# Last expert layer: rows of the routed tiles moved between partition quarters by plain transfers and transposed by VectorE in 32x32 blocks

## The chip, the cores and the metric

The kernel runs on one core of one Trainium2 chip. The metric is the device time of one execution in microseconds. Of the kernel before, four runs are given: 1134.13, 1129.19, 1130.49 and 1135.69 us, with a median of 1132.31 us. One more execution was profiled; it took 1130.32 us.

A core has five engines that run side by side, each with its own queue of instructions: TensorE (PE, matrix products and transposes into PSUM), VectorE (DVE), ScalarE (ACT), GpSimd (POOL) and SyncE (SP). Work passes between them by semaphores. Sixteen DMA engines move data between HBM and SBUF or inside SBUF. Transfers are issued from SP's queue, or, where rows are picked by an index, from POOL's.

## The reference

The program is two decoder layers of a gated cross-attention model on x of shape (4, 512, 512) in float32, that is 2048 tokens of width 512. Each layer adds a gated cross-attention and then a gated mixture of experts, both on a layer norm of x. Only the second mixture of experts, the last step, is touched by the change. Cut to what matters:

```python
x = hidden_states.reshape(-1, 512)                 # 2048 tokens
probs = softmax(x @ router_w.T)                    # 8 experts
topk_w, topk_idx = top_k(probs, 2)
topk_w = topk_w / sum(topk_w)
combine = zeros((2048, 8)).at[token, topk_idx].add(topk_w)
for e in range(8):                                 # gw, uw: 512 x 352, dw: 352 x 512
    out = silu(x @ gw[e]) * (x @ uw[e]) @ dw[e]
    acc = acc + combine[:, e, None] * out
shared = silu(x @ s_gate_w + b) * (x @ s_up_w + b) @ s_down_w + b
result = acc + shared
```

So each token goes through two of eight experts, and through a shared expert beside them. The kernel computes a token only at its two experts.

## The kernel before

**How the layer is tiled.** The 4096 pairs of token and expert are sorted by expert on the chip, and each expert's list is cut into tiles of 128 rows. `NTS` = 36 tiles are computed in a fixed loop; three more (`NT4` = 39) stand behind a branch that is taken only if the routing needs them. Which tokens a tile holds is known only at run time, so its rows are fetched by index: `gat4` holds the row numbers, `put4` the places where the results go.

**A tile's steps.** `rows4(i)` has POOL gather 128 rows of 512 values from HBM (`h4_dram`, the normed x) into the tile `xr`. A product on TensorE needs the 512 values along the partitions, so `in4(i)` transposes: the helper `transposed` runs four 128x128 transposes on TensorE into the PSUM tile `ptr` (L245) and copies them with one ScalarE instruction into `xrT` (L246). `up4(i)` multiplies `xrT` with the gate and the up weights (`pgr` and `pur`, L1443; four chunks of 128 each, which the profile shows as eight matmuls of 352 columns), takes silu on ScalarE (L1445) and multiplies on VectorE with the token's weight (`sgr`, L1446). `turn4(i)` transposes the result on TensorE (`pti`, L1454). `down4(i)` multiplies with the down weights (`por`, L1463), adds half the shared expert's bias on VectorE (`yr`, L1465) and scatters the rows from POOL (L1466).

**Weights.** Three buffers (`NW` = 3) hold an expert's gate, up and down weights (`wbuf`). `weights4(i)` gathers them from POOL by index in two transfers of 128 rows, of 11.3 KB and of 6.1 KB. Where tile i has the same expert as tile i - 3, the index lies out of bounds and nothing is moved.

**What sets the order.** TensorE and VectorE follow the order of the program text in this stage (a schedule by hand); the order on POOL, ScalarE and SP comes from a scheduler when the kernel is built, and is fixed from then on. In iteration i of the loop TensorE gets `up4(i + 1)`, the transposes of `in4(i + 2)`, `down4(i)` and `turn4(i + 1)`. Ahead of the loop stand the gathers of tiles 0 to 3, `in4(0)`, `up4(0)`, the third weight buffer, `in4(1)` and `turn4(0)`. SP issues nothing between the read of the slot table (`tab`, L1401) and the load of the shared expert's second half (L716, L717) at the end of the loop. After the loop come the sums of each token's two rows (L1517) and the rest of the shared expert (L1201, L1217).

**Memory.** Tiles come from pools. `row` buffers (nine of 2 KB per partition) hold `xr` and `yr`; `xrT` has three buffers. The pool `c4` holds, for the stage between the two expert layers, seven buffers `yk` of the first layer's gathered rows and the keys and values `kb` and `vb`; `wd2` and `half_db` take `yk` buffers over.

**Weight layout.** On the host `k_major` lays a weight out so that partition p of chunk c holds input value 128 c + p, to match the transposes.

Of the kernel before, what the change touches and what calls it, by code (L numbers as in the profile page):

```python
# [9 lines left out]
F32 = mybir.dt.float32  # L10
# [7 lines left out]
P = 128  # L18
B, S, D = 4, 512, 512
T = B * S  # L20
NT = T // P
TB = S // P
DC = D // P
N = 64
KSET = 4
HEADS = 16
HD = D // HEADS
# [6 lines left out]
E1, I1 = 8, 352  # L34
NT4 = (2 * T + E1 * (P - 1)) // P
NTS = 2 * T // P + E1 // 2
# [4 lines left out]
NROW = 9  # L41
NYK = 7
NW = 3
WROW = 2 * DC * I1
# [21 lines left out]
def flamingo_gated(  # L66
# [8 lines left out]
    nc = tc.nc  # L75
    V, A, G, PE = nc.vector, nc.scalar, nc.gpsimd, nc.tensor
# [4 lines left out]
    work = ctx.enter_context(tc.tile_pool(name="work", bufs=2))  # L81
# [9 lines left out]
    h4_dram = dram.tile([T, D], F32, name="h4_dram")  # L91
# [27 lines left out]
    for g in range(B):  # L119
# [22 lines left out]
        out=tri, in_=ones, compare_op=ALU.is_gt, fill=0.0, base=0,  # L142
# [98 lines left out]
    def transposed(dst, src, name, part=slice(0, P)):  # L241

        pt = ps_t.tile([P, DC, P], F32, name=name, tag="pt")
        for c in range(DC):
            PE.transpose(pt[:, c, :], src[:, c * P : (c + 1) * P], ident)  # L245
        A.copy(dst, pt[:, :, part])  # L246
# [479 lines left out]
    weights, rows0, xbTs, sgs, its = {}, {}, {}, {}, {}  # L726
# [128 lines left out]
    for i in range(NT2):  # L855
# [4 lines left out]
        k = i // 4 + 2  # L860
# [25 lines left out]
    c4 = ctx.enter_context(tc.tile_pool(name="c4", bufs=1))  # L886


    sm4 = ctx.enter_context(tc.tile_pool(name="sm4", bufs=2))


    TURN = [2, 0, 3, 1]
# [26 lines left out]
    for h in range(2):  # L919
        G.affine_select(  # L920
            out=cmask[h * N : (h + 1) * N, :], in_=ones[h * N : (h + 1) * N, :N], compare_op=ALU.is_ge,
# [22 lines left out]
        )  # L944

    def fetch(t, k):
        yk = c4.tile([P, D], F32, name=f"yk{t}_{k}", tag="yk", bufs=NYK)
        G.indirect_dma_start(  # L948
            out=yk,
            out_offset=None,  # L950
            in_=y_dram[:, :],
            in_offset=bass.IndirectOffsetOnAxis(ap=rows_of[:, t, k : k + 1], axis=0),
            bounds_check=NSLOT + P - 1,
            oob_is_err=False,
        )
        return yk
# [128 lines left out]


    def keys3(b):
        kb = c4.tile([P, DC, 4, N], F32, name=f"kb{b}", tag="kb", bufs=2)
        vb = c4.tile([P, HEADS // 2, 2, HD], F32, name=f"vb{b}", tag="vb", bufs=2)
        nc.sync.dma_start(out=kb, in_=kblk[b])  # L1090
        nc.sync.dma_start(out=vb, in_=vblk[b])
        return kb, vb

    pairs3 = [(2 * pair, 2 * pair + 1) for pair in range(2)]
    kv3 = {b: keys3(b) for b in pairs3[0]}
    loop.close()
    by_hand.close()
# [142 lines left out]
    def step(gen, n=1):  # L1240
        for _ in range(n):
            next(gen)
# [135 lines left out]
    def gather(out_, src, idx, n):  # L1378
        G.indirect_dma_start(
            out=out_,  # L1380
            out_offset=None,
            in_=src[:, :],
            in_offset=bass.IndirectOffsetOnAxis(ap=idx, axis=0),
            bounds_check=n - 1,
            oob_is_err=False,
        )
# [4 lines left out]
    def weights4(i):  # L1391
        wgu, wd = views4(at4[i])
        gather(wgu.rearrange("p a c i -> p (a c i)"), wgu1, wrow[:, i : i + 1], E1 * P)
        gather(wd.rearrange("p c d -> p (c d)"), wd1, wrow[:, i : i + 1], E1 * P)
# [13 lines left out]
    gat4 = c4.tile([P, NT4], I32, name="gat4")  # L1408
# [7 lines left out]
    run(d1)  # L1416


    wd2 = c4.tile([P, D], F32, name="wd2", tag="yk", bufs=NYK)
    nc.sync.dma_start(out=wd2, in_=wsd1[IS[0] + 2 * P :, :])  # L1420
    half_db = c4.tile([P, D], F32, name="half_db", tag="yk", bufs=NYK)
    nc.sync.dma_start(out=half_db, in_=sdb1.partition_broadcast(P))
    V.tensor_scalar(half_db, half_db, gf[:, 1:2], 0.5, ALU.mult, ALU.mult)

    xrs, xrTs, sgs, its = {}, {}, {}, {}

    def rows4(i):
        xrs[i] = work.tile([P, D], F32, name=f"xr{i}", tag="row", bufs=NROW)  # L1430
        gather(xrs[i], h4_dram, gat4[:, i : i + 1], T)

    def in4(i):
        xrTs[i] = work.tile([P, DC, P], F32, name=f"xrT{i}", tag="xnT", bufs=3)
        transposed(xrTs[i], xrs.pop(i), f"ptr{i}")

    def up4(i):
        (wgu, _), xbT = views4(at4[i]), xrTs.pop(i)
        pg = ps.tile([P, I1], F32, name=f"pgr{i}", tag="g")
        pu = ps.tile([P, I1], F32, name=f"pur{i}", tag="u")  # L1440
        for a, p_ in enumerate((pg, pu)):
            for c in range(DC):
                PE.matmul(p_, lhsT=xbT[:, c, :], rhs=wgu[:, a, c, :], start=(c == 0), stop=(c == DC - 1))  # L1443
        sg = work.tile([P, 512], F32, name=f"sgr{i}", tag="sg")
        A.activation(sg[:, :I1], pg, AF.Silu)  # L1445
        V.scalar_tensor_tensor(sg[:, :I1], pu, slots[:, 1, i : i + 1], sg[:, :I1], ALU.mult, ALU.mult)  # L1446
        sgs[i] = sg
# [28 lines left out]
        tc.add_to_no_dep_group("y4", d.ins)  # L1476

    after = [shared4(1, W5, g, wd2) for g in range(B)]
    for i in range(4):
        rows4(i)  # L1480
    in4(0)
    up4(0)
    weights4(NW - 1)
    in4(1)
    turn4(0)
    for i in range(NTS):
        if i + 1 < NTS:
            up4(i + 1)
        if i + 2 < NTS:
            in4(i + 2)  # L1490
        if i + 4 < NTS:
            rows4(i + 4)
        if i + 1 == NTS:
            step(after[0])
        down4(i)
        if i + NW < NTS:
            weights4(i + NW)
        elif i + NW == NTS:
            load_shared4(1, W5)
        if i + 1 < NTS:  # L1500
            turn4(i + 1)
# [20 lines left out]
def _host_layout(i):  # L1522
    import numpy as np

    def k_major(w):
        w = np.asarray(w)
        *lead, k, m = w.shape
        w = w.reshape(*lead, k // P, P, m)
        return np.ascontiguousarray(np.moveaxis(w, -3, -2))

    def t(w):
        return np.swapaxes(np.asarray(w), -1, -2)

    def beside(g, u):
        return np.concatenate([t(g), t(u)], axis=-1)

    def by_chunk(v):
        v = np.asarray(v)
        v = np.concatenate([v[: IS[0]], v[IS[0] - P // 2 :]])
        return np.ascontiguousarray(v.reshape(2, 3, P).transpose(2, 0, 1))  # L1540

    def shared1(part):
        return np.stack([k_major(np.asarray(i[f"L1_ffn_s_{n}_w"])[:, part]) for n in ("gate", "up")], axis=1)

    c = np.ascontiguousarray
    ctxs = np.asarray(i["ctx_2048"])

    kblk = np.zeros((B, 4, HD, DC, 4, N), ctxs.dtype)
    vblk = np.zeros((B, 2, N, HEADS // 2, 2, HD), ctxs.dtype)
    for j in range(4):  # L1550
        kblk[:, j, :, :, j] = ctxs.reshape(B, N, DC, 4, HD)[:, :, :, j].transpose(0, 3, 2, 1)
    for j in range(2):
        vblk[:, j, :, :, j] = ctxs.reshape(B, N, HEADS // 2, 2, HD)[:, :, :, j]
    kblk = kblk.reshape(B, P, DC, 4, N)
    vblk = vblk.reshape(B, P, HEADS // 2, 2, HD)
    return {
        "x": c(np.asarray(i["x"]).reshape(T, D)),

        "xT": c(np.asarray(i["x"]).reshape(B, TB, P, DC, P).transpose(1, 4, 3, 0, 2).reshape(B, P, DC, S)),
        "ctx": c(ctxs),  # L1560
        "kblk": c(kblk),
        "vblk": c(vblk),
        "itok": c(np.asarray(i["itok_Sx4_0_63"])),
        "g_xattn": c(np.asarray(i["g_xattn"])),
        "g_ffn": c(np.asarray(i["g_ffn"])),
        "descT": k_major(t(i["L0_xattn_desc_router"])),
        "w_q": c(np.asarray(i["L0_xattn_W_q"])),
        "b_q": c(np.asarray(i["L0_xattn_b_q"]).reshape(DC, P).T),
        "gate0T": k_major(t(i["L0_ffn_gate_w"])),
        "bias0": c(np.asarray(i["L0_ffn_bias"])),  # L1570
        "wgu0": k_major(beside(i["L0_ffn_w_gate"], i["L0_ffn_w_up"])),
        "wd0": k_major(t(i["L0_ffn_w_down"])),
        "wsgu0": k_major(beside(i["L0_ffn_sg"], i["L0_ffn_su"])),
        "wsd0": k_major(t(i["L0_ffn_sd"])),
        "gate1T": k_major(t(i["L1_ffn_router_w"])),
        "wgu1": c(
            np.stack([k_major(i["L1_ffn_gate_w"]), k_major(i["L1_ffn_up_w"])], axis=2).reshape(E1 * P, WROW)
        ),
        "wd1": k_major(
            np.pad(np.asarray(i["L1_ffn_down_w"]), ((0, 0), (0, 3 * P - I1), (0, 0)))  # L1580
        ).reshape(E1 * P, 3 * D),
        "wsgu1a": shared1(slice(0, IS[0])),
        "wsgu1b": shared1(slice(IS[0], IS[0] + IS[1])),
        "wsd1": c(np.asarray(i["L1_ffn_s_down_w"])),
        "sgb1": by_chunk(i["L1_ffn_s_gate_b"]),
        "sub1": by_chunk(i["L1_ffn_s_up_b"]),
        "sdb1": c(np.asarray(i["L1_ffn_s_down_b"])),
    }
# [19 lines left out]
```

## Time and profile before

| what | value |
|---|---|
| median of four runs | 1132.31 us (1129.19 to 1135.69) |
| profiled execution, its own time | 1130.32 us |
| its span, first to last instruction | 1127.8 us |
| mean granted TensorE clock | 0.948 |
| TensorE busy | 1022.5 us, 91% |
| VectorE, ScalarE, GpSimd busy | 446.8, 228.6, 375.7 us |
| transposes of the gathered rows (L245, ptr) | 144, from 707.0 to 986.3 us |
| routed products (L1443, L1463) | from 708.3 to about 1007 us |
| DMA, mean over the span | 190 GB/s |

The profile is one execution on the chip. Its busy table gives each engine's share of the span. A timeline lists instructions in order of time: start, duration, engine, line, operation, output and inputs, how many were merged, and in brackets the idle time before and what ended it. Matmuls overlap, so a row's duration is longer than the distance to the next; distances between starts are the better measure. A table of windows gives for stretches of time the busy time of each engine (with the number of instructions), the granted clock, the share of time that the 16 DMA engines were busy, and GB/s. For a line or a tile, a summary lists durations (shortest, median, longest in ns) and the first and last start.

### The profile page before, as it was taken

The page shows a single profiled execution, that of the slowest core. Times are in us where ns is not written, and L with a number is a line of the kernel's source. Part 1 is how long each engine was busy: PE and PEld are TensorE (multiplying, and loading weights), DVE is VectorE, ACT ScalarE, POOL GpSimd, SP SyncE. Part 2 cuts the span into 40 slices and gives each one's busy share as a digit, 9 for nine tenths or more (in the row PEclk, how much of TensorE's full clock was granted, in tenths as well). Part 3 has the DMA queues.
Part 4 walks back from the last instruction along what each step waited for, and adds up shares of the span by engine and source line. Part 5 has one row for each costly group of instructions (what it writes and reads, how often), then busy time and mean ns, then how long its engine had stood idle before and what let it go on. Part 6 is the DMA issues. An engine that isn't in the chain of part 4 may idle for free. (4 is left out here: it accounts for less than half of the span.)

```text
span 1127.8 us, 10977 instructions
## 1 busy us (share of the span) xinstructions
PE 1022.5 (91%) x3462; PEld 505.3 (45%) x3462; DVE 446.8 (40%) x1212; ACT 228.6 (20%) x489; POOL 375.7 (33%) x412
## 2 busy tenths in 40 slices
PE   4479889999999999799586699999999999999998
PEld 2134434444444444334243444565656565644443
DVE  5989946232232322375856343111111111118111
ACT  1144111222222222023232300121212111110000
POOL 2001142333222340466624443454545454410000
PEclk7679899999999999899878599999999999999999
DMA  8512137788887786755624406576577787338100
GB/s 321 224 75 78 32 100 238 239 289 282 285 280 253 266 286 219 265 173 166 201 93 147 39 1 167 175 261 235 186 266 267 279 285 253 140 128 309 38 37 37
DMA packets 67994, 214.70 MB, mean 190 GB/s; under 512 B 16958, under 2 KB 18014, under 8 KB 59744
## 3 DMA queue, kind: packets, MB, share of 16 engines
q0 software_dynamic: 28608, 107.81, 30.2%
q1 hardware_dynamic: 37024, 101.99, 25.0%
q10 hardware_dynamic: 2304, 4.20, 1.9%
q8 instruction: 28, 0.46, 0.2%
q14 instruction: 30, 0.25, 0.1%
HBM read 206.16 MB, written 35.57 MB: 214 GB/s over the span
## 5 line engine op out<-in xcount | busy, mean ns | idle before, releaser
L788 PE MATMUL gu<-wbuf,xbT 128*128 128x512 f32 (+1 forms) x512 | 174.0, 596 | 1.0 <-issue 0.7
L948 POOL DMA_INDIRECT yk<-y_dram,rows_of x76 | 83.7, 1101 | 107.9 <-DVE x L965 52.2
L770 POOL DMA_INDIRECT xb<-h_dram,get x48 | 48.1, 1003 | 165.6 <-issue 97.3
L1463 PE MATMUL por<-wbuf,itr 128*128 128x512 f32 (+1 forms) x216 | 98.7, 593 | 0.0
L788 PEld LDWEIGHTS gu<-wbuf,xbT 128*128 128x128 f32 (+1 forms) x512 | 63.1, 163 | 78.0 <-issue 77.3
L795 DVE SCALAR_TENSOR_TENSOR sgb<-gu,xb,sgb 128x256 f32<-128x256 f32 (+1 forms) x64 | 30.9, 483 | 158.4 <-ACT sgb L793 117.2
L1443 PE MATMUL pgr<-wbuf,xrT 128*128 128x352 f32 x288 | 91.3, 460 | 0.7 <-ACT xrT L246 0.7
L813 PE MATMUL pob<-wbuf,itb 128*128 128x512 f32 (+1 forms) x256 | 91.2, 599 | 0.0
L1443 PE MATMUL pur<-wbuf,xrT 128*128 128x352 f32 x288 | 91.1, 459 | 0.0
L1201 PE MATMUL pg<-lnT,wbuf 128*128 128x512 f32 (+1 forms) x224 | 85.0, 559 | 0.5 <-PEq L1505 0.5
L1446 DVE SCALAR_TENSOR_TENSOR sgr<-pur,slots,sgr 128x352 f32<-128x352 f32 x36 | 21.0, 584 | 161.3 <-PE pur L1443 125.4
L1201 PE MATMUL pu<-lnT,wbuf 128*128 128x512 f32 (+1 forms) x224 | 79.6, 532 | 1.9 <-DVE it L1207 1.9
L1466 POOL DMA_INDIRECT y_dram<-yr,put x36 | 37.3, 1037 | 110.2 <-DVE yr L1465 105.6
L1443 PEld LDWEIGHTS pur<-wbuf,xrT 128*128 128x128 f32 x288 | 54.7, 190 | 30.5
L1217 PE MATMUL po<-wbuf,it 128*128 128x512 f32 x128 | 63.3, 629 | 4.2 <-DVE x L1227 2.5
L1443 PEld LDWEIGHTS pgr<-wbuf,xrT 128*128 128x128 f32 x288 | 51.9, 190 | 23.8 <-ACT xrT L246 0.9
L1465 DVE TENSOR_TENSOR yr<-por,half_db 128x512 f32<-128x512 f32 x36 | 24.9, 692 | 91.0 <-PE por L1463 91.0
L748 POOL DMA_INDIRECT found<-cnt_dram,look x48 | 48.4, 1007 | 26.3 <-issue 14.3
L1201 PEld LDWEIGHTS pg<-lnT,wbuf 128*128 128x128 f32 (+1 forms) x224 | 35.7, 183 | 45.4 <-issue 43.6
L1463 PEld LDWEIGHTS por<-wbuf,itr 128*128 128x128 f32 (+1 forms) x216 | 38.5, 191 | 35.1 <-issue 34.9
L1201 PEld LDWEIGHTS pu<-lnT,wbuf 128*128 128x128 f32 (+1 forms) x224 | 34.9, 175 | 42.8 <-issue 38.0
L818 DVE COPY y<-pob 128x512 f32<-128x512 f32 x48 | 33.2, 692 | 44.6 <-PE pob L813 29.6
(394 smaller groups left out, 1310.6 us busy)
## 6 DMA issues: line engine op xcount, KB each, us to landing
wbuf<-in_wgu_dram SPq DMA_DIRECT2D x32, 1024.0 KB
wbuf<-in_wd_dram SPq DMA_DIRECT2D x32, 512.0 KB
y_dram<-y SPq DMA_DIRECT2D x48, 256.0 KB
y<-y_dram SPq DMA_DIRECT2D x32, 256.0 KB
lnT<-in_xT_dram SPq DMA_DIRECT2D x4, 1024.0 KB
x<-in_x_dram SPq DMA_DIRECT2D x16, 256.0 KB
h_dram<-h SPq DMA_DIRECT2D x16, 256.0 KB
h_dram<-xn ACTq DMA_DIRECT2D x16, 256.0 KB
```

What stands on the lines that cost most here:

```text
L748: G.indirect_dma_start(out=found[k][:, j, :], out_offset=None, in_=cnt_dram[:, :], in_offset=bass.IndirectOffsetOnAxis(ap=look2[:, i : i + ...
L770: G.indirect_dma_start(out=rows0[i], out_offset=None, in_=h_dram[:, :], in_offset=bass.IndirectOffsetOnAxis(ap=get2[:, i : i + 1], axis=0) ...
L788: PE.matmul(gu[p_, :], lhsT=xbT[:, c, p_], rhs=weights[e][0][:, c, :], start=(c == 0), stop=(c == DC - 1),)
L795: V.scalar_tensor_tensor(sg[p_, :I0], gu[p_, I0:], xb[p_, D + e : D + e + 1], sg[p_, :I0], ALU.mult, ALU.mult)
L813: PE.matmul(po[p_, :], lhsT=it[:, ic, p_], rhs=weights[e][1][:, ic, :], start=(ic == 0), stop=(ic == I0 // P - 1),)
L818: V.tensor_copy(y, po)
L948: G.indirect_dma_start(out=yk, out_offset=None, in_=y_dram[:, :], in_offset=bass.IndirectOffsetOnAxis(ap=rows_of[:, t, k : k + 1], axis=0) ...
L1201: PE.matmul(p_[m, :n], lhsT=wgu[:, a, c, i], rhs=lnT[g][:, c, k], start=(c == 0), stop=(c == DC - 1))
L1217: PE.matmul(po, lhsT=it[:, ic, k * P : (k + 1) * P], rhs=wd[:, ic, :] if ic < 2 else wd2, start=(ic == 0), stop=(ic == 2),)
L1443: PE.matmul(p_, lhsT=xbT[:, c, :], rhs=wgu[:, a, c, :], start=(c == 0), stop=(c == DC - 1))
L1463: PE.matmul(po, lhsT=it[:ni, ic, :], rhs=wd[:ni, ic, :], start=(ic == 0), stop=(ic == 2))
L1466: d = G.indirect_dma_start(out=y4_dram[:, :], out_offset=bass.IndirectOffsetOnAxis(ap=put4[:, i : i + 1], axis=0), in_=yr, in_offset=None, ...
```

## The change

For tiles 4 to 35 the transposes of the gathered rows leave TensorE.

- `pair_rows4(i)` gathers the rows of two tiles into one tile `rp` (three buffers). Then 16 plain transfers from SP's queue, each of 32 partitions by two tiles by 128 values, copy `rp` to `q` (two buffers): quarter r of each row, from partition quarter a, goes to partition quarter r, place a. Now each 32x32 block lies in the partitions in which its transpose belongs.
- `in4_blocks(i)` is one VectorE instruction that transposes the sixteen 32x32 blocks of a tile from `q` into `xrT`. It stands where `in4` stood in the program text.
- Partition 32 r + j of chunk c now holds input value 128 r + 32 c + j. The gate and up weights are laid out to match on the host (`by_32`).
- Tiles 0 to 3 (`BYPE` = 4), and the tiles behind the branch, are still transposed by TensorE. They need the same order, so `in4` first copies the rows on ScalarE into a permuted tile `x32`.
- Pairs 4 and 6 are gathered ahead of the loop; pair i + 6 is asked for in each even iteration i.
- `yk`, `kb` and `vb` move to a pool `between`, which is closed before the layer; `rp`, `q`, `wd2` and `half_db` take its place in a pool `d4`.

```diff
-        yk = c4.tile([P, D], F32, name=f"yk{t}_{k}", tag="yk", bufs=NYK)
+        yk = between.tile([P, D], F32, name=f"yk{t}_{k}", tag="yk", bufs=NYK)
...
-    wd2 = c4.tile([P, D], F32, name="wd2", tag="yk", bufs=NYK)
+    scope3.close()
+    d4 = ctx.enter_context(tc.tile_pool(name="d4", bufs=1))
+    wd2 = d4.tile([P, D], F32, name="wd2")
...
+    B4 = P // 32
...
     def in4(i):
         xrTs[i] = work.tile([P, DC, P], F32, name=f"xrT{i}", tag="xnT", bufs=3)
-        transposed(xrTs[i], xrs.pop(i), f"ptr{i}")
+        x32 = work.tile([P, DC, B4, 32], F32, name=f"x32_{i}", tag="row", bufs=NROW)
+        A.copy(x32, xrs.pop(i).rearrange("p (r c d) -> p c r d", r=B4, c=DC))
+        transposed(xrTs[i], x32.rearrange("p c r d -> p (c r d)"), f"ptr{i}")
+
+    def pair_rows4(i):
+        rp = d4.tile([P, 2, D], F32, name=f"rp{i}", tag="rp", bufs=3)
+        for j in range(2):
+            gather(rp[:, j, :], h4_dram, gat4[:, i + j : i + j + 1], T)
+        q = d4.tile([P, 2, B4, P], F32, name=f"q{i}", tag="q", bufs=2)
+        for a in range(B4):
+            for r in range(DC):
+                nc.sync.dma_start(
+                    out=q[32 * r : 32 * r + 32, :, a, :], in_=rp[32 * a : 32 * a + 32, :, r * P : (r + 1) * P]
+                )
+        for j in range(2):
+            xqs[i + j] = q[:, j]
+
+    def in4_blocks(i):
+        xrTs[i] = work.tile([P, DC, P], F32, name=f"xrT{i}", tag="xnT", bufs=3)
+        V.transpose(
+            out=xrTs[i].rearrange("p c (a t) -> p a c t", a=B4),
+            in_=xqs.pop(i).rearrange("p a (c t) -> p a c t", t=32),
+        )
...
-    for i in range(4):
+    BYPE = 4
+    for i in range(BYPE):
         rows4(i)
+    for i in range(BYPE, BYPE + 4, 2):
+        pair_rows4(i)
...
         if i + 2 < NTS:
-            in4(i + 2)
-        if i + 4 < NTS:
-            rows4(i + 4)
+            (in4 if i + 2 < BYPE else in4_blocks)(i + 2)
+        if i % 2 == 0 and BYPE + 4 <= i + 6 < NTS:
+            pair_rows4(i + 6)
...
+    def by_32(w):
+        w = np.asarray(w)
+        *lead, k, m = w.shape
+        w = w.reshape(*lead, P // 32, k // P, 32, m)
+        return np.ascontiguousarray(np.moveaxis(w, -3, -2).reshape(*lead, P, k // P, m))
...
-            np.stack([k_major(i["L1_ffn_gate_w"]), k_major(i["L1_ffn_up_w"])], axis=2).reshape(E1 * P, WROW)
+            np.stack([by_32(i["L1_ffn_gate_w"]), by_32(i["L1_ffn_up_w"])], axis=2).reshape(E1 * P, WROW)
```

## The prediction

> **What bounds the kernel now.** I read the busy table, then a timeline of the last expert layer, then its windows by tile, then single transfers.
>
> ```profile
> PE 1022.5 (91%) x3462; PEld 505.3 (45%) x3462; DVE 446.8 (40%) x1212; ACT 228.6 (20%) x489; POOL 375.7 (33%) x412
> ```
>
> TensorE is busy for 91% of the span. One tile of the last expert layer in the timeline (start, duration, engine):
>
> ```profile
> 889.00 0.60 PE L245 MATMUL ptr<-ident,xr 128*128 128x128 f32 x4
> 889.27 0.58 DVE L1446 SCALAR_TENSOR_TENSOR sgr<-pur,slots,sgr 128x352 f32<-128x352 f32 x1 [4.44 <-PE pur L1443]
> 889.44 2.74 PE L1463 MATMUL por<-wbuf,itr 128*128 128x512 f32 x6
> 892.02 0.49 PE L1454 MATMUL pti<-ident,sgr 128*128 128x128 f32 x3
> 892.22 0.69 DVE L1465 TENSOR_TENSOR yr<-por,half_db 128x512 f32<-128x512 f32 x1 [2.36 <-PE por L1463]
> 892.35 2.53 PE L1443 MATMUL pgr<-wbuf,xrT 128*128 128x352 f32 x8
> 894.72 2.53 PE L1443 MATMUL pur<-wbuf,xrT 128*128 128x352 f32 x8
> 897.08 0.60 PE L245 MATMUL ptr<-ident,xr 128*128 128x128 f32 x4
> ```
>
> A tile takes 897.08 - 889.00 = 8.08 us, and no PE line shows idle time: TensorE alone sets this pace, at granted clock 1.00. From the first ptr to the first por is 889.44 - 889.00 = 0.44 us (0.43 elsewhere). VectorE idles 2.37 us between sgr's end (889.85) and yr.
>
> The DMA engines are the next resource. Four successive tiles of one expert; the last two columns are DMA share and GB/s:
>
> ```profile
> 843.23:851.31 8.08, 8.08 (x31) 4.85 (x30) 1.28 (x2) 1.58 (x4) 4.05 (x4) 1.00 0.77 248
> 851.31:859.39 8.08, 8.08 (x31) 4.85 (x30) 1.28 (x2) 1.58 (x4) 4.05 (x4) 1.00 0.88 322
> 859.39:867.48 8.09, 8.09 (x31) 4.86 (x30) 1.28 (x2) 1.58 (x4) 4.06 (x4) 1.00 0.91 331
> 867.48:875.56 8.08, 8.08 (x31) 4.85 (x30) 1.28 (x2) 1.58 (x4) 4.06 (x4) 1.00 0.50 175
> ```
>
> An expert's first three tiles load weights, the rest reuse them. This group averages 0.765 x 8.08 = 6.18 us of engine time a tile. The dips in share read as five groups of four tiles and three of five; the five at 754 to 795 average 0.65, or 5.3 us.
>
> **The change, part by part.**
>
> *PE transposes removed.* 32 tiles lose four ptr each: 32 x 0.435 = 13.9 us. They lie on the path, since PE has no gaps; the period becomes 7.65 us. Their 32 ScalarE evictions (0.59 each) were off it: worth nothing.
>
> *Block transpose added on VectorE* (32, each between sgr and yr). The trace has none. Nearest rows: DVE passes over 128x512 f32, 0.69 us; the low end is sgr's 0.58, the high end two passes, 1.4. I take 0.69. With ptr gone, pgr of that tile starts 892.35 - 0.44 - 889.85 = 2.06 us after sgr: all three fit, cost 0. Queued behind it on VectorE are yr, its scatter on POOL and the next sgr, so a transpose waiting for its rows stops PE about 2 us later.
>
> *256 plain transfers added on SP* (16 a pair of tiles, 32 KB each; 512 KB a pair). SP's queue is otherwise empty between the slot table (692) and the shared weights (987): nothing is overtaken. An issue is 0.33 to 0.46 us there: 16 x 0.36 = 5.8 us per 15.3 us pair. Each waits for the one eight before it, so eight are in flight. A pair's fill begins when the block transposes two pairs earlier have freed its buffer, and must end three periods later: 22.9 us. The price of landing under weight loads:
>
> ```profile
> L1401 SPq DMA_DIRECT2D tab<-slot_dram x1: 327/327/327, 692.1 to 692.1; - x1
> L1404 PE MATMUL pslot<-pick,tab x4: 287/300/367, 700.1 to 700.5; 128*128 128x39 f32 x4
> ```
>
> The 128 KB table, behind two tiles' weight gathers, is used 8.0 us after issue (7.7 after its end). A first gather of counts with little beside it is used 2.0 us after its instruction. Two rounds of eight are 4 to 15.4 us; both fit 22.9. Cost 0, taken nearer the high end, because weights are in flight here too.
>
> A rule speaks against this. The Trainium skill (DMA: Bandwidth & Descriptors, Rules for kernel authors) says that transfers under 64 KB are mostly overhead, and its page SBUF — State Buffer (The DMA setup-cost knee) gives each about 2 us that does not shrink with its bytes. Paid one after the other, that makes an estimated 16 x 2 = 32 us a pair, 16.7 over the 15.3, some 270 us slower in all. The table row shows a landing even longer than the rule's, but eight that are in flight together share it, so the sum goes by the row.
>
> *Engine time of those transfers.* 512 pieces of 512 B a tile, 32 per DMA engine:
>
> ```profile
> 112.00:114.00 2.00, 2.00 (x6) 0.95 (x5) 1.82 (x6) 0.50 (x1) 0.00 (x0) 1.00 0.45 70
> 146.00:148.00 2.00, 2.00 (x6) 0.93 (x5) 0.00 (x0) 0.40 (x1) 1.40 (x3) 1.00 0.29 33
> 1020.00:1030.00 10.00, 10.00 (x25) 4.46 (x24) 9.73 (x16) 0.00 (x0) 0.00 (x0) 1.00 1.01 367
> ```
>
> Router weights in 128 B pieces: 0.45 x 16 x 2 us over 140 KB = 13 ns each. Count gathers in 512 B rows: 9.3 us over 66 KB = 72 ns. y loads in 2 KB rows: 90 ns. Between the plain ones a 512 B piece is 13 + 384/1920 x 77 = 28 ns; the gather row, indirect and from HBM, is the nearest in size and the high end. I take 35 ns, since these are plain and stay in SBUF: 1.1 us a tile. A four-tile group then needs 6.18 + 1.1 = 7.3 of 7.65 us: hidden, cost 0. The margin is 1.47 us, or 46 ns a piece. At 72 ns (2.3 us) it is gone; see the first rival.
>
> *Row gathers in pairs.* As many as before. Their tiles have three buffers and POOL is busy 4.05 of 8.08 us: cost 0.
>
> *Start of the layer.* The first four tiles stay on PE, with an added ScalarE copy each:
>
> ```profile
> 705.29 1.00 POOL L1379 DMA_INDIRECT xr<-h_dram,gat  x1 [0.30 <-PE po L1217]
> 707.69 0.59 ACT L246 COPY xrT<-ptr 128x512 f32<-128x512 f32 x1 [12.91 <-PE ptr L245]
> 708.33 2.63 PE L1443 MATMUL pgr<-wbuf,xrT 128*128 128x352 f32 x8 [0.68 <-ACT xrT L246]
> ```
>
> In the instruction order of the changed kernel ScalarE does three such copies before xrT of tile 0, and the third needs the third gather (705.29 above). It lands at 706.3 + 2.0 = 708.3; two ACT passes of 0.59 put the first pgr at 709.6, 1.3 us late; with the table's landing it would be 7 us late. I take 1.5, as only 1 MB of rows stands in line. Four more row gathers (1.3 each) also push tile 2's weight gather from 707.9 to 713.1. At 6.3 us of load and 2.0 landing it is there by 722; tile 2 needs it at 722.6 + 1.5. Cost 0, up to 2 if late.
>
> *Weights stored in another row order, pool moved:* same bytes, same queue order before the layer: 0.
>
> Sum: -13.9 + 1.5 = -12.4 us. The profiled execution took 1130.3 (span 1127.8), so 1117.9; it lies 2.0 below the median of the runs, 1132.3. Against that: 1120.
>
> **Rivals.**
>
> 1. *The DMA engines become the bound (slower).* Place: the 20 tiles in groups of four. Price: at 72 ns a tile needs 8.48 us, 0.83 over 7.65, 17 us over 20 tiles, net +4: 1137. At 90 ns: 9.08 us, 29 us, plus 15 tiles of the five-tile groups at 0.5, 8 us: net +24, 1156. It decides from 65 ns a piece, where the excess is 12 us. For it: shares of 0.88 to 0.91 in loading tiles. Against: 13 ns for small plain pieces.
> 2. *Rows late without full engines (gain lost, no change).* If a round of eight must wait out a tile's whole load (0.9 x 8.08 = 7.3 us) and then land (3.3, between 2.0 and 7.7), with 2.9 us for issue, two rounds take 24.1 us, 1.2 over the window. At ten loaded pairs that is 12 us: 1132. For it: the table's 8 us. Against: that table had eight 1 KB pieces per engine, these have four of 512 B.
> 3. *VectorE transposes far slower than a pass.* Above 2.06 us the excess is on the path: at four passes (2.8) 0.7 x 32 = 22 us, 1142. Against: every 128x512 f32 pass here is 0.7 or less.
>
> **How the numbers follow.** Clean overlap 0.66, 1115 to 1124 (start 0 to 5 us, up to 2 us of scattered stalls, 2 us between medians). Rival 2 0.10, 1124 to 1134. Rival 1 0.20, 1133 to 1160. Rival 3 0.04. A median of this kernel can tell about 0.5%, 5.7 us, from no change: faster is below 1126.6. Faster: 0.66 + 0.02. Slower (above 1138): three quarters of rival 1 and rival 3, 0.19. Same: 0.13. The range 1114 to 1140 leaves about 0.17 above and little below. Clean overlap alone: 1115 to 1124.
>
> **What would show it.** Right: a 7.65 us tile with no PE idle, DMA share near 0.95 in a four-tile group, the transpose near 0.7 us, the first pgr some 1.5 us after ptr ends. Wrong: PE waiting at pgr for the block transpose and that for q; periods above 8.08 in loading tiles only (rival 1 if DMA share is 1.0, rival 2 if it is lower); a transpose above 2 us in every tile (rival 3).

## The result: the gain is there for fourteen tiles, then it is given back

| | kernel before | kernel after |
|---|---|---|
| median | 1132.45 us (73 runs) | 1135.74 us (47 runs) |
| ratio | 1 | 1.0032, interval 1.0023 to 1.0042 |
| profiled execution | 1130.32 us | 1135.53 us |
| its span | 1127.8 us | 1133.8 us |
| first routed product to the last one (start of pgr of tile 0 to that of tile 35) | 281.01 us | 285.16 us |

Where 1120 us was forecast, the kernel is 0.3% slower than before, inside the 0.5% that the prediction took for no change. The last row of the table is called the layer's length below; it leaves out what lies before the layer, which varies by some microseconds between executions.

The busy table after. ScalarE and TensorE have less work, VectorE more, as announced:

```profile
PE 1014.2 (89%) x3334; PEld 495.4 (44%) x3334; DVE 467.1 (41%) x1244; ACT 212.1 (19%) x461; POOL 374.9 (33%) x412
```

Windows of the kernel after, from one start of pgr to the next: length, busy time of PE, PEld, DVE, ACT and POOL, granted clock, DMA share, GB/s. The first two are tiles early in the layer, the third one of the second half:

```profile
739.95:747.60 7.65, 7.65 (x28) 4.47 (x27) 1.90 (x4) 1.00 (x3) 5.05 (x5) 1.00 0.96 338
755.24:762.88 7.64, 7.64 (x27) 4.46 (x26) 1.89 (x4) 1.00 (x3) 4.06 (x4) 1.00 0.85 273
857.14:866.33 9.19, 7.88 (x25) 4.47 (x26) 1.90 (x3) 1.00 (x3) 5.09 (x6) 1.00 0.97 344
```

The early tiles take the 7.65 us that the sum was built on, without a gap on TensorE and with the DMA engines 85 to 96% busy. The late tile takes 9.19, of which TensorE is busy for 7.88. The timeline of pgr shows where this begins (start, duration, and in brackets the idle time before and what ended it):

```profile
816.39 2.53 PE L1472 MATMUL pgr<-wbuf,xrT 128*128 128x352 f32 x8
824.61 2.60 PE L1472 MATMUL pgr<-wbuf,xrT 128*128 128x352 f32 x8 [0.41 <-DVE yr L1494]
832.32 2.53 PE L1472 MATMUL pgr<-wbuf,xrT 128*128 128x352 f32 x8
840.34 2.61 PE L1472 MATMUL pgr<-wbuf,xrT 128*128 128x352 f32 x8 [0.21 <-DMA wbuf<-in_wgu_dram,wrow]
848.05 2.53 PE L1472 MATMUL pgr<-wbuf,xrT 128*128 128x352 f32 x8
857.14 2.60 PE L1472 MATMUL pgr<-wbuf,xrT 128*128 128x352 f32 x8 [1.28 <-DMA wbuf<-in_wgu_dram,wrow]
866.33 2.60 PE L1472 MATMUL pgr<-wbuf,xrT 128*128 128x352 f32 x8 [1.32 <-DMA wbuf<-in_wgu_dram,wrow]
```

At tile 14 (816.39) the kernel is 3.2 us ahead of the kernel before, whose tile 14 begins at 819.61. From there it loses up to 2 us in more than every second tile; the first wait of TensorE above 0.5 us is that of tile 19 (857.14). The waits of the layer, by what ended them (total us, times, longest):

```profile
PEld pgr L1472 <- issue: 12.3, 14, 2.6
PE pgr L1472 <- DMA wbuf<-in_wgu_dram,wrow: 11.0, 11, 1.8
PEld pgr L1472 <- DVE yr L1494: 7.9, 6, 1.5
DVE yr L1494 <- DMA q<-rp: 2.4, 1, 2.4
DVE xrT L1461 <- DMA q<-rp: 0.8, 1, 0.8
```

The weight loads (PEld) and the products (PE) of pgr stall at the same places. TensorE waits for gate and up weights, a transfer that the change does not touch; for the moved rows there are only two waits on VectorE, of 2.4 and 0.8 us. GpSimd's own timeline tells why. Before:

```profile
846.04 1.02 POOL L1379 DMA_INDIRECT wbuf<-in_wd_dram,wrow  x1 [0.31 <-issue]
847.37 1.01 POOL L1379 DMA_INDIRECT xr<-h_dram,gat  x1 [0.30 <-issue]
849.03 0.99 POOL L1379 DMA_INDIRECT wbuf<-in_wgu_dram,wrow  x1 [0.66 <-PE pur L1443]
852.78 1.04 POOL L1466 DMA_INDIRECT y_dram<-yr,put  x1 [2.77 <-DVE yr L1465]
```

After:

```profile
835.82 1.00 POOL L1381 DMA_INDIRECT wbuf<-in_wgu_dram,wrow  x1 [0.30 <-issue]
840.81 1.03 POOL L1495 DMA_INDIRECT y_dram<-yr,put  x1 [3.99 <-DVE yr L1494]
842.14 1.01 POOL L1381 DMA_INDIRECT wbuf<-in_wd_dram,wrow  x1 [0.31 <-DMA q<-rp]
843.46 1.02 POOL L1381 DMA_INDIRECT rp<-h_dram,gat  x1 [0.30 <-issue]
844.78 1.01 POOL L1381 DMA_INDIRECT rp<-h_dram,gat  x1 [0.31 <-issue]
848.90 1.03 POOL L1495 DMA_INDIRECT y_dram<-yr,put  x1 [3.11 <-DVE yr L1494]
850.23 1.02 POOL L1381 DMA_INDIRECT wbuf<-in_wgu_dram,wrow  x1 [0.30 <-issue]
851.55 1.00 POOL L1381 DMA_INDIRECT wbuf<-in_wd_dram,wrow  x1 [0.30 <-issue]
```

Before, the gather of the next gate and up weights goes out as soon as the tile that held the buffer has finished pur (849.03), and the tile that needs them begins at 868.10: 19.1 us later. After, from the middle of the layer on, the same gather stands behind the scatter of y, which waits for yr of the tile three before the one that needs the weights. It goes out at 850.23 and its tile is held until 857.14: 6.9 us. Nothing in the edit asks for this; the order on GpSimd is the scheduler's, and in the kernel after it is another. In the first half of the layer it was still the old one, with the gate and up gather (835.82) ahead of the scatter (840.81).

So there were two questions: what this order costs by itself, and whether the transfers cost anything.

### The profile page after: what moved, and what is told of

Same layout as the page of the kernel before. It is cut to its first block, busy times and chain, and to the rows that moved or that the text cites. A ratio compares the mean times of both kernels' runs of the same rounds, so it can differ in the third digit from the quotient of the medians.

```text
span 1133.8 us, 11060 instructions
## 1 busy us (share of the span) xinstructions
PE 1014.2 (89%) x3334; PEld 495.4 (44%) x3334; DVE 467.1 (41%) x1244; ACT 212.1 (19%) x461; POOL 374.9 (33%) x412
## 3 DMA queue, kind: packets, MB, share of 16 engines
q1 hardware_dynamic: 57504, 110.40, 28.3%
## 5 line engine op out<-in xcount | busy, mean ns | idle before, releaser
L1472 PE MATMUL pgr<-wbuf,xrT 128*128 128x352 f32 x288 | 94.0, 470 | 15.6 <-DMA wbuf<-in_wgu_dram,wrow 11.0
L1495 POOL DMA_INDIRECT y_dram<-yr,put x36 | 36.9, 1024 | 120.2 <-DVE yr L1494 109.8
L1492 PEld LDWEIGHTS por<-wbuf,itr 128*128 128x128 f32 (+1 forms) x216 | 41.0, 190 | 41.9 <-issue 34.9
L1209 DVE SCALAR_TENSOR_TENSOR it<-pu,ub_sb,sg 128x512 f32<-128x512 f32 (+1 forms) x24 | 16.9, 704 | 83.0 <-PE pu L1203 66.6
```

The lines of the kernel that those rows point to most:

```text
L1492: PE.matmul(po, lhsT=it[:ni, ic, :], rhs=wd[:ni, ic, :], start=(ic == 0), stop=(ic == 2))
L1495: d = G.indirect_dma_start(out=y4_dram[:, :], out_offset=bass.IndirectOffsetOnAxis(ap=put4[:, i : i + 1], axis=0), in_=yr, in_offset=None, ...
```

## The experiments

Each experiment's ratio is against runs of the kernel before on the same chip. "Layer" is the length defined above, from the profiled execution; e5 and e9, the same kernel on two chips, differ by 2.2 us in it.

| run | ratio and interval | layer |
|---|---|---|
| before | 1 | 281.01 |
| after | 1.0032 (1.0023 to 1.0042) | 285.16 |
| e1 early order | 1.0022 (1.0003 to 1.0041) | 284.35 |
| e2 late order | 1.0141 (1.0100 to 1.0182) | 300.80 |
| e3 early, no transfers | 0.9891 (0.9865 to 0.9917) | 268.66 |
| e4 late, no transfers | 1.0129 (1.0095 to 1.0162) | 297.37 |
| e5 early, deeper | 0.9908 (0.9882 to 0.9933) | 268.65 |
| e6 early, long pieces | 0.9917 (0.9888 to 0.9945) | 268.65 |
| e7 before, late order | 1.0170 (1.0133 to 1.0207) | 296.10 |
| e8 early, deeper, mended start | 0.9893 (0.9867 to 0.9920) | 267.83 |
| e9 as e5, beside e8 | 0.9927 (0.9903 to 0.9951) | 270.86 |

**e1 to e4: the order and the transfers, one by one.** The first theory was that the order alone makes the difference, the second that the transfers do. `weights4` is split into `gate_up4` and `down_w4`, and GpSimd's order in the loop is written out by hand. Early (e1) is the order of the kernel before:

```diff
+    gate_up4(NW)
     for i in range(NTS):
         if i + 1 < NTS:
             up4(i + 1)
+        if i + 1 + NW < NTS:
+            gate_up4(i + 1 + NW)
...
         down4(i)
         if i + NW < NTS:
-            weights4(i + NW)
+            down_w4(i + NW)
...
+        if i % 2 == 0 and BYPE + 4 <= i + 6 < NTS:
+            pair_rows4(i + 6)
```

> The changed kernel with the order of POOL's queue written out: the gate and up weights of tile i + 4 are asked for ahead of the scatter of tile i, as in the kernel before, instead of those of tile i + 3 behind it. Transfers and block transposes are unchanged. Theory A (order on POOL: in the changed kernel's trace the weight gather of a tile is issued at 850.23, behind the scatter at 848.90, and its tile starts 1.28 us late at 857.14, so it has about 6 us where the kernel before gives about 19): the waits for weights, about 17 us from 824 us on, go, and the time falls from 1135.7 to about 1119. Theory B (the 256 transfers take DMA time away from the weights): the waits stay, 1131 or more.

Late (e2) keeps `weights4(i + NW)` behind `down4(i)` for all tiles, with `pair_rows4` after it.

> The changed kernel with the late order (scatter of tile i, then the weights of tile i + 3, then the row gathers) written out for all tiles; in the changed kernel it begins at about tile 15. Theory A: tiles 4 to 14 now wait too, some 0.5 to 1 us each where weights are loaded (6 of 11 tiles): 1139 to 1142. Theory B: the same as the changed kernel, 1134 to 1137.

e3 and e4 are the same two without the 256 transfers; the block transpose reads the gathered rows directly, so the products are of other numbers:

```diff
-        q = d4.tile([P, 2, B4, P], F32, name=f"q{i}", tag="q", bufs=2)
-        for a in range(B4):
-            for r in range(DC):
-                nc.sync.dma_start(...)
         for j in range(2):
-            xqs[i + j] = q[:, j]
+            xqs[i + j] = rp[:, j].rearrange("p (a t) -> p a t", a=B4)
```

> As the early order, but the 256 transfers are left out: the block transposes read the gathered rows where they lie, so the rows of tiles 4 to 35 reach the products with their quarters in the wrong places. Both theories: no waits for weights, 1117 to 1119. Beside the early order with transfers it gives what the transfers cost: 0 to 2 us by theory A, 12 or more by theory B.

> The late order for all tiles without the transfers (the same part left out). Theory A: the gathers still start too late, 1126 to 1138. Theory B: with no transfers beside them the weights land in time, 1117 to 1120.

Before took 1126.03 us on that chip. e1 took 1129.53, e2 1143.34, e3 1112.98, e4 1142.45 us. The wait that costs TensorE most in the layer of e4, with no transfer at all:

```profile
PE pgr L1473 <- DMA wbuf<-in_wgu_dram,wrow: 21.9, 14, 2.8
```

and in e1, with the early order and all transfers:

```profile
DVE xrT L1468 <- DMA q<-rp: 17.7, 6, 6.6
PE pgr L1479 <- DVE xrT L1468: 10.4, 4, 5.2
```

Neither theory stands alone. The late order makes the weights late whether rows are moved or not: it adds 28.7 us to the layer without transfers (297.37 - 268.66), more than either theory allowed for. With the early order no tile waits for gate and up weights, but now the moved rows are late, and that loses 15.7 us (284.35 - 268.66), more than the first theory left for it. Only without both is the gain there, and e3's 1.1% is a little less than was expected (1117 to 1119 beside 1132.45 is 1.2 to 1.4%; the interval measured is 0.83 to 1.35%). The two losses do not add up: under the late order the transfers cost 3.4 us (300.80 - 297.37), presumably since a tile that is held by weights gives them more time. That fits the profile of after, which shows almost no wait for q.

The pair of e1 that is latest, tiles 32 and 33, in the timeline. A row of SP merges transfers; the two rows come from neighbouring windows, and the ninth transfer, issued at 945.79, stands in both:

```profile
931.82 1.00 POOL L1381 DMA_INDIRECT rp<-h_dram,gat  x1 [0.30 <-issue]
938.58 7.82 SPq L1460 DMA_DIRECT2D q<-rp  x9
945.79 8.25 SPq L1460 DMA_DIRECT2D q<-rp  x8
963.48 0.71 DVE L1468 STREAM_TRANSPOSE xrT<-q 128x512 f32<-128x512 f32 x1 [6.65 <-DMA q<-rp]
964.25 5.06 PE L1479 MATMUL pgr<-wbuf,xrT 128*128 128x352 f32 x8 [5.20 <-DVE xrT L1468]
```

The rows are in place at 938.58, when the first transfer goes out. The sixteenth is issued by 954.04, 0.97 us apiece. The last has landed when VectorE starts at 963.48: 24.9 us after the rows, and 31.7 us after the first gather. VectorE was ready for them at 963.48 - 6.65 = 956.83. The semaphore updates in the trace give the same for every pair, from the first issue to the last landing: 13.4 to 24.6 us, with a median of 18.0, so this pair is the longest of the sixteen. How long an issue takes on SP (shortest, median, longest in ns), and what SP waited for before one:

```profile
L1460 SPq DMA_DIRECT2D q<-rp x256: 585/595/2132, 708.0 to 968.4; - x128
SPq L1460 <- DMA rp<-h_dram,gat: 70.0, 15, 18.6
SPq L1460 <- DMA q<-rp: 35.9, 40, 2.1
```

In 15 pairs the fill begins when the gathered rows land. After that each issue takes 0.6 us, and 40 of them also wait for an earlier transfer to land. While the sixteen of the pair above were issued, and then until they had landed, the windows show:

```profile
938.58:945.79 7.21, 7.21 (x25) 4.19 (x24) 1.89 (x3) 0.94 (x3) 2.62 (x4) 1.00 0.96 318
945.79:953.46 7.67, 7.67 (x27) 4.49 (x26) 1.90 (x3) 1.00 (x3) 5.09 (x6) 1.00 0.95 317
953.46:963.17 9.71, 5.59 (x19) 2.90 (x17) 0.58 (x1) 1.00 (x3) 1.99 (x2) 0.97 0.80 291
```

The DMA engines were 95 to 96% busy during the issues and 80% while the last transfers landed.

**e5: the same transfers, begun 15.3 us sooner.** A third buffer q, and the pair of tile i + 8 asked for in place of i + 6. `wd2` moves into a buffer `rp` after the last pair, to make room.

```diff
-        q = d4.tile([P, 2, B4, P], F32, name=f"q{i}", tag="q", bufs=2)
+        q = d4.tile([P, 2, B4, P], F32, name=f"q{i}", tag="q", bufs=3)
...
-        if i % 2 == 0 and BYPE + 4 <= i + 6 < NTS:
-            pair_rows4(i + 6)
+        if i % 2 == 0 and BYPE + 6 <= i + 8 < NTS:
+            pair_rows4(i + 8)
```

> The early order of GpSimd's queue, all 256 transfers, and each pair of tiles fetched two tiles sooner (three buffers q in place of two; the shared expert's last weights move into a buffer rp after the last pair). Theory A: in the early-order run with transfers the only waits left were for q (17.7 us on VectorE, 6 times), because the sixteen transfers of a pair needed 24.8 us from rows in place (938.58) to the last landing (about 963.4) and the lead was shorter; 15.3 us more lead ends these waits. Then the time is that of the early order without transfers, less what the engines' added load costs: ratio 0.989 to 0.993, that is 1113 to 1118 us where before is 1126. Theory B: the DMA engines (share 0.90 in most stretches of that run) are themselves the pace; the lead is eaten up in the first third of the layer and the waits come back: ratio 0.998 to 1.004.

Measured: 1118.57 us where before took 1128.52, ratio 0.9908. No wait for q is left, and the layer takes 268.65 us, the same as without any transfer (268.66). Two windows of e5 in the loading half of the layer:

```profile
836.00:868.00 32.00, 32.00 (x106) 18.77 (x105) 7.58 (x12) 4.01 (x13) 17.35 (x18) 1.00 0.95 315
868.00:900.00 32.00, 32.00 (x105) 18.62 (x104) 8.43 (x14) 3.98 (x12) 17.30 (x18) 1.00 0.94 320
```

TensorE has no gap although the DMA engines are 94 to 95% busy, more than in e1 (0.89 to 0.90 in the same windows). The transfers are no faster than in e1: a pair takes 13.2 to 24.6 us from the first issue to the last landing, with a median of 19.5. The engines are not the bound at this load; the start of the transfers was too late.

**e6: half the pieces, the same bytes, and other transfers for each tile.** Why does a pair take so long? Either the bytes and the transfers take their time, or each piece waits its turn. e6 is e1 with 32 pieces of 1024 bytes in a transfer in place of 64 of 512. The values land in wrong places, so the products are of other numbers.

```diff
+        qf, rf = (t.rearrange("p j a t -> p (j a t)") for t in (q, rp.rearrange("p j (a t) -> p j a t", a=B4)))
         for a in range(B4):
             for r in range(DC):
                 nc.sync.dma_start(
-                    out=q[32 * r : 32 * r + 32, :, a, :], in_=rp[32 * a : 32 * a + 32, :, r * P : (r + 1) * P]
+                    out=qf[32 * r : 32 * r + 32, 2 * P * a : 2 * P * a + 2 * P],
+                    in_=rf[32 * a : 32 * a + 32, 2 * P * r : 2 * P * r + 2 * P],
                 )
```

> The early order with the same 256 transfers of 32 KB, between the same tiles and partitions, but each made of 32 pieces of 1024 bytes in place of 64 of 512; the parts of the rows land in wrong places, so the products are of other numbers. Bytes, transfers and order are the same. Theory A: a piece waits its turn behind the packets of the weight gathers, so the landing goes by the number of pieces; 32 pieces an engine for eight transfers took 7.2 to 9.7 us, 16 would take about 4 to 5, two rounds 8 to 10, and no tile waits for rows: ratio 0.989 to 0.993. Theory B: the landing goes by bytes, or each transfer takes its time whatever it holds: it stays at 7 to 10 us a round and the ratio at 1.000 to 1.004.

Measured: 1119.48 us, ratio 0.9917, layer 268.65, no wait for q. The ratio is that of the first theory, but the experiment does not show its mechanism, for the edit changes a second thing. A piece of 1024 bytes is two pieces of one tile, where e1's transfer holds one piece for each tile of the pair. So in e6 the first eight transfers fill the first tile of the pair and the last eight the second; in e1 both tiles need all sixteen. The traces agree: in e1 only the block transpose of a pair's first tile waits for the transfers' semaphores, in e6 that of each tile does. Tile 32 of e6 is transposed at 953.14, while the last transfer of its pair lands at 957.00; in the pairs of tiles 14 and 16 too the last landing lies behind the first transpose, by 1.6 and 1.3 us. Had those three first tiles needed all sixteen, they would have waited.

The first theory also expected rounds of 4 to 5 us. By the semaphore updates, as a mean of the sixteen pairs:

| us from a pair's first issue to | e1 | e6 |
|---|---|---|
| the ninth issue | 6.5 | 6.3 |
| the landing of the first eight | 11.1 | 10.8 |
| the landing of all sixteen | 18.0 | 17.1 |

With half the pieces a pair is 5% shorter, not half as long. In those three pairs, then, it was the other order that ended the wait; in the rest no run separates it from the shorter pieces. The issue on SP is hardly shorter (here e6), and the queue's engine time over the whole span hardly less (packets, MB, share of 16 engines; e1, then e6):

```profile
L1461 SPq DMA_DIRECT2D q<-rp x256: 507/589/2300, 711.2 to 962.4; - x128
q1 hardware_dynamic: 57504, 110.40, 28.4%
q1 hardware_dynamic: 49312, 110.40, 28.5%
```

What makes a transfer land late under the weights stays open. The Trainium skill (DMA: Bandwidth & Descriptors, Queues, rings and completion order) says that each DMA engine goes round between the queues with work and switches only at packet boundaries, a packet being typically 9 to 17 descriptors. By that a transfer could wait for a whole turn of the weights whatever the size of its own pieces; no run here shows it.

**e7: the order alone, in the kernel before.** TensorE's transposes stay; GpSimd's order is the late one.

```diff
-        if i + 4 < NTS:
-            rows4(i + 4)
         if i + 1 == NTS:
             step(after[0])
         down4(i)
         if i + NW < NTS:
             weights4(i + NW)
         elif i + NW == NTS:
             load_shared4(1, W5)
+        if i + 4 < NTS:
+            rows4(i + 4)
```

> The kernel before, with TensorE's transposes, but GpSimd's queue in the order that the changed kernel had from the layer's middle on (scatter of y, the two weight gathers of three tiles ahead, then the row gather), written out for all tiles. Theory A: this order alone makes the weights late, as it did with and without the transfers (+29 us between the two orders without transfers, at 7.65 us a tile); at 8.08 us a tile somewhat less: ratio 1.008 to 1.025. Theory B: it is late only together with the paired row gathers, whose two in a row put 2.6 us in front of a weight gather: ratio 0.998 to 1.003.

Measured: 1147.07 us where before took 1128.52, ratio 1.0170, layer 15.1 us longer. TensorE's waits for gate and up weights, and one of its stalls:

```profile
PE pgr L1443 <- DMA wbuf<-in_wgu_dram,wrow: 6.7, 9, 1.2
910.30 2.61 PE L1443 MATMUL pgr<-wbuf,xrT 128*128 128x352 f32 x8 [1.20 <-DMA wbuf<-in_wgu_dram,wrow]
```

Six more waits of pgr, 3.9 us in all, are put down to ScalarE (itr). The kernel before has no idle time of TensorE above 0.15 us from 720 us to the end of the layer.

So the order needs neither the paired gathers nor the shorter tile to cost time. It is a price of its own, which the change brought along by way of the scheduler.

**e8 and e9: the start of the layer.** e9 is e5 again, on the same chip as e8. In e8 the copy of tile 0's rows stays on ScalarE and those of tiles 1 to 3 go to VectorE:

```diff
+    order4(0, A.copy)
     in4(0)
+    for i in range(1, BYPE):
+        order4(i, V.tensor_copy)
     up4(0)
```

> The deeper-prefetch kernel with the start of the layer mended: the copy of tile 0's row stays on ScalarE, those of tiles 1 to 3 go to VectorE ahead of its first product, so that no copy that waits for a later tile's rows stands in front of the transposed block of tile 0. In the deeper-prefetch run the first product of the layer waited 2.79 us for that block and its eight matmuls then took 4.33 us, where the kernel before waited 0.68 and took 2.63 us. Theory A: the copies are the cause: the wait falls to 0.7 to 1.5 us, the eight matmuls to 2.6 us, and the kernel gains 1 to 4 us on the deeper-prefetch kernel: ratio 0.986 to 0.991 of before. Theory B: the first rows themselves arrive late, and the copies only stand beside that: no gain, ratio as for the deeper-prefetch kernel beside it within 0.001.

> The deeper-prefetch kernel once more, on the same chip as the one with the mended start and with more rounds: ratio 0.988 to 0.993 by either theory; its distance to the mended one is the price of the start.

Measured: e8 1122.85, e9 1125.78 us, where before took 1134.68. The first products of e9:

```profile
714.07 2.63 PE L1477 MATMUL pgr<-wbuf,xrT 128*128 128x352 f32 x8 [2.06 <-ACT x L1446]
722.39 4.33 PE L1477 MATMUL pgr<-wbuf,xrT 128*128 128x352 f32 x8 [2.02 <-issue]
```

and of e8:

```profile
711.98 2.63 PE L1482 MATMUL pgr<-wbuf,xrT 128*128 128x352 f32 x8 [0.67 <-ACT xrT L246]
718.11 2.62 PE L1482 MATMUL pgr<-wbuf,xrT 128*128 128x352 f32 x8
727.07 2.60 PE L1482 MATMUL pgr<-wbuf,xrT 128*128 128x352 f32 x8 [0.64 <-ACT itr L1495]
```

The wait for the first block is 0.67 us, as in the kernel before (0.68), and the slow products are gone. The layer is 3.0 us shorter and the medians lie 2.9 us apart; the two intervals overlap a little, so the size is less sure than the mechanism. e8 is the fastest version that computes the reference: 11.8 us below before on its chip, where the prediction's sum was 12.4.

## Why the prediction was wrong

Right, by its own steps:

- *PE transposes removed, 13.9 us, and the 7.65 us tile.* The early tiles take 7.64 to 7.65. Without waits (e5) the stretch from tile 3 to tile 35 takes 244.58 us, where before takes 258.63: 14.1 us less. The whole layer is 12.4 us shorter (268.65 against 281.01), because its first three tiles take 1.7 us longer in e5; with the start mended (e8) it is 13.2 us shorter.
- *Block transpose, 0.69 us, cost 0.* 0.70 us, and never the cause of a wait when its rows were there; the third rival is out:

```profile
L1461 DVE STREAM_TRANSPOSE xrT<-q x32: 700/702/712, 737.8 to 992.8; 128x512 f32<-128x512 f32 x32
```

- *Engine time, 35 ns a piece.* The records of single packets in the trace of after give 28.7 ns for a piece of 512 bytes. The queue's share rose from 25.0% of 1127.8 to 28.3% of 1133.8 us, 38.9 us per engine for 32 tiles or 1.2 us a tile; that is 38 ns a piece, with the 4-byte packets that go with them and with whatever the queue's other loads took longer. Hidden, as e5 shows. The first rival, to which 0.20 was given, is out: it needed 65 ns.
- *Start of the layer, 1.5 us late.* In the profile of after the first pgr waits 2.32 us where it waited 0.68, 1.6 us more. In e5 that wait was 2.79 us and its eight matmuls then took 4.33 us, which the step did not have.

Wrong, and each enough by itself to take the gain (e1 against e3, e4 against e3):

- *"Row gathers in pairs ... POOL is busy 4.05 of 8.08 us: cost 0."* This step looked at GpSimd's load and not at its order. What counts on a queue with spare time is which instruction stands behind which wait. The gate and up gather moved behind the scatter of y, and its lead fell from 19.1 to 6.9 us. From tile 3 to tile 35 after takes 262.61 us, 18.0 more than e5; of the 13.3 us that TensorE stands idle there, 11.0 end with these weights. For "pool moved" the step says "same queue order before the layer"; inside the layer no step looked at that of GpSimd. No rival had this mechanism, so the text would have been wrong even with the second part right.
- *"Two rounds of eight are 4 to 15.4 us; both fit 22.9. Cost 0 ..."* Both numbers failed. In e1 a pair took 13.4 to 24.6 us, with a median of 18.0. A single landing was mostly shorter than the table's 7.7 us (from the end of its issue 4.6 us in the median, 10.4 at most); what the two rounds left out is the issuing. An issue took 0.6 us in place of 0.36, and with the waits for earlier transfers the sixteen issues alone took 10.9 to 15.5 us in place of 5.8; the landing of the last comes on top. The window was no 22.9 us either: 16.5 to 21.1 us in the five pairs that were more than 1 us late (18.2 in the one shown), because the fill began not when the buffer came free but when the gathered rows landed. The sign is that of the second rival, rows late with the engines short of full (0.89 to 0.90 over long stretches of e1, up to 0.96 in the pair shown). Its 12 us of loss compares with 15.7 in e1, but that is partly luck: its 24.1 us for two rounds is right only for the longest pair, and its window was 22.9 too. It had 0.10. In after itself it is hidden behind the late weights.

The rule that the prediction weighed, that of small transfers which are mostly overhead, was set aside for the table's row. Sixteen transfers took up to 24.6 us, between the 15.4 of the high end and the estimate of 32 that would follow if nothing overlapped. The table row was a single transfer; it said nothing of what it costs to issue sixteen in a row.

What stays open: why the scheduler changed its order in the middle of the layer, and what makes a transfer of 32 KB take some 5 us to land beside the weights. A test of the piece size alone would keep, for each tile, the transfers that it needs.

## What to carry to other kernels

When an edit adds gathers to a queue that a scheduler orders, read the new order of that queue through the whole stage, and for each load the time from its issue to its use; spare time on the engine says nothing about it. Many small transfers in a row have to be begun earlier than their bytes suggest while large ones are in flight: here 512 KB in sixteen transfers took 13 to 25 us, and a third buffer, at no cost that the runs show, returned all of the gain. Two faults that hide each other need both to be taken away before either shows, so test them crosswise. When an experiment changes the shape of a transfer, look which transfers each reader now waits for, before a shorter time is put down to the shape.

## What the runs showed of the hardware

**The clock drops after short waits, and not by their length alone.** In e1 the product after a wait of 5.20 us took 5.06 us for its eight matmuls, in place of 2.53. Windows of e1, the granted clock being the third number from the end:

```profile
880.00:884.00 4.00, 3.21 (x6) 1.96 (x7) 1.29 (x2) 0.00 (x0) 2.06 (x2) 0.57 0.76 278
964.00:968.00 4.00, 3.75 (x7) 2.26 (x8) 0.77 (x2) 0.00 (x0) 2.05 (x2) 0.50 0.32 91
972.00:976.00 4.00, 4.00 (x15) 2.20 (x14) 1.75 (x3) 0.53 (x2) 1.65 (x2) 1.00 0.02 0
```

After that wait TensorE runs at half its clock for some 5 us, which adds about 2.5 us to the wait itself. A wait of 2.47 us (before 880.79) did it too, in e9 one of 2.02 us, and in after one of 1.79 us:

```profile
970.22 4.30 PE L1472 MATMUL pgr<-wbuf,xrT 128*128 128x352 f32 x8 [1.79 <-DMA wbuf<-in_wgu_dram,wrow]
```

But 2.32 us at the layer's start in after and 2.19 us in e4 (before 942.27) did not: their eight matmuls took 2.63 and 2.60 us. The Trainium skill (TensorE: Matmul & The Clock Gate, Part 1: The HAM clock gate) gives half the clock after an idle window of about 3.4 us that runs freely; the half is what the trace shows, but waits shorter than the window were enough here. The other waits inside the layer of after were not followed by it (2.60 us for the eight matmuls), so its loss is mostly waiting (13.3 of 18.0 us).

**A plain piece of 1024 bytes costs the engines a little less than two of 512.** In the packet records of the layer a piece of 1024 bytes takes 50.5 ns in e6 and one of 512 bytes 28.8 ns in e1.
